# Two attention stages of a six-stage decoder on one core: layernorms cut into steps, a scale moved from the softmax sums into a copy, and one routing job sent at a time

## The chip, the cores and the metric

The kernel runs as one program on one core of a Trainium2 chip. The core has a matrix engine (PE, with its weight loads shown as PEld), a vector engine (DVE), a scalar engine (ACT), a GpSimd engine (POOL), a queue engine that starts most transfers (SP), and 16 DMA engines. Each engine takes its own instructions in order, and semaphores tie the engines together. The metric is the device time of one execution in microseconds (us); the smaller the better.

## What is computed

The reference is a post-norm decoder of two layers over x of 16 blocks x 128 tokens x 512 features: a state-space scan, a cross attention, a ternary feed-forward, a bit-linear self attention, a gated cross attention, and a mixture of experts. Each is followed by a residual sum and a layernorm:

```python
x = _layernorm(x + _L0_attn_ref(x, ...))      # scan
x = _layernorm(x + _L0_xattn_ref(x, ctx, ...))
x = _layernorm(x + _L0_ffn_ref(x, ...))
x = _layernorm(x + _L1_attn_ref(x, ...))      # 16 heads of 32, ternary weights, 8-bit activations
x = _layernorm(x + _L1_xattn_ref(x, ctx, mask, ...))   # 16 heads of 32, gated
x = _layernorm(x + _L1_ffn_ref(x, ...))       # 64 experts in 8 groups, top 8
```

The change lies in the fourth and fifth. The fifth, cut to what matters:

```python
q, k, v = heads of rmsnorm(x) @ wq.T, memory @ wk.T, memory @ wv.T
attn = softmax(where(mask, q k^T / sqrt(32), -inf));  attn = nan_to_num(attn, nan=0)
out  = (attn @ v) @ wo.T
return sigmoid(x @ wg.T) * out
```

A block whose memory tokens are all masked gives 0, which the kernel gets from a flag per block (`gated_any`, a [128, 16] tile named anyk in the profile). The sigmoid is computed as (1 + tanh) / 2, so a factor of one half stands somewhere in the kernel.

## The kernel before

Six stages follow one another: scan, cross attention, feed-forward, then `stage_attention`, which holds both small-head attentions, and `stage_moe`.

**The attention stage.** x lies in 16 tiles of 128 tokens (x0 to x15), taken in pairs. There are 8 pairs of `SelfAttention` and then 8 of `GatedAttention`, and each pair is worked in 8 units of four heads of a tile, 128 units in all. The loop at L1518 takes one step t per unit. Around step t it issues, for units at different lags: the score matmuls (`scores`, two steps ahead), the row maxima (`top`, one step ahead, L1442 and L1443 on DVE), the exponentials (`exps`, L1451 on ACT, four per unit, with their sums into sm), the division by the sums (`norm`, one step behind), the turn of the probabilities (`turn`: PE transposes pts at L536, and a copy at_T, on ACT at L1295 or on DVE at L1297), and after each four units the generator `values` of the tile. Generators are in the list `running`, and each is advanced once per step: `project` (transposes pt of x and the copies xT at L1380 and L1383 on DVE, queries, copy qT at L1411, gate at L1415 and L1420 on ACT), `values`, weight loads.

**One unit's division in the gated attention** (`norm`, L1455): DVE takes the reciprocal of sm, 128x4 (L1457), DVE multiplies it by the block's flag and by 0.5 (L1459), and POOL multiplies the 128x512 tile at_s by it (L1460).

**A tile's end in the gated attention** (`values`, L1464): PE makes ao from at_T and v (L1472), ACT copies it to oT (L1478), PE multiplies by the output weights into pw (L1482), DVE makes gate = (gate + 1) * pw (L1485), and POOL adds it to x (L1486). After the second tile of a pair, the layernorm of both tiles runs as one block (L1490): bn_stats (L101) and bn_aggr (L102) for both tiles, a reciprocal square root by Newton steps (L78 to L91), and two 128x512 multiplications (L105). Its instructions are given to a scheduler by `keep_in_program_order`.

**The order of instructions.** A scheduler of the framework places each engine's instructions before the program is built; what `keep_in_program_order` wraps keeps its place relative to the other wrapped instructions of the engine, the rest may move. So the order on an engine is fixed when the program runs, and an instruction whose input is late holds all behind it on its engine.

**Routing beside the gated attention.** When a pair of tiles of the first half has its layernorm, its number is appended to `to_route` (L1493). `Moe.tick`, called twice a step, advances one `route` job: transposes of x, gate logits, top 8, softmax and offsets, a chain of small DVE operations (L1675 to L1751). A routed pair then becomes a job of `sending`. `Moe.send`, called once a step, advances every job of that list: each advance issues two scatters of rows by POOL (L1760, an indirect DMA; 16 per pair, so 64 in all beside the attention). POOL thus carries L1460, L1486 and L1760 in one queue.

**Tiles with few buffers.** The transposes pts and pt share one PSUM buffer (`ppt`, bufs=1), ao and pw share one (`pao`), at_s has four.

**The experts.** `stage_moe` (from about 2183 us) runs the routed rows through gate, up and down matmuls; it calls `m.send` once a step for the pairs that were not sent before.

Of the kernel before, what the change touches and what calls it, by code (L numbers as in the profile page):

```python
# [10 lines left out]
F32 = mybir.dt.float32  # L11
BF16 = mybir.dt.bfloat16
F32R = mybir.dt.float32r
I32 = mybir.dt.int32
# [6 lines left out]
P = 128  # L21
# [11 lines left out]
class Homes:  # L33


    def __init__(self, **homes):
        self.homes = homes
# [57 lines left out]
def layernorm(k, ins, outs, eps=1e-5, keep=lambda ins: ins):  # L95

    nc, n = k.nc, len(ins)
    mv = k.small.tile([P, n, 2], F32, tag=f"ln_mv{n}", name="ln_mv")
    for i, r in enumerate(ins):
        st = k.small.tile([P, nc.vector.BN_STATS_DIM], F32, tag="ln_st", name="ln_st")  # L100
        keep(nc.vector.bn_stats(st, r))  # L101
        keep(nc.vector.bn_aggr(mv[:, i, :], st))  # L102
    rstd = rsqrt(k, mv[:, :, 1], n, eps, keep=keep)
    for i, (r, o) in enumerate(zip(ins, outs)):
        keep(nc.vector.tensor_scalar(o, r, mv[:, i, 0:1], rstd[:, i : i + 1], ALU.subtract, ALU.mult))  # L105


def stage_ssm(k):
# [981 lines left out]
def load_gated_masks(k, raws):  # L1090


    nc, a, pool = k.nc, k.args, k.bit_pool
    m8 = raws.tile([P, NB, P], U8, name="m8")
    nc.sync.dma_start(m8, a["mask"].rearrange("b t -> (b t)").partition_broadcast(P).rearrange("p (b t) -> p b t", b=NB))
    yield
    k.gated_any = pool.tile([P, NB], F32, name="anyk")
    k.tc.keep_in_program_order(nc.vector.tensor_reduce(k.gated_any, m8, AX.X, ALU.max))
    yield
    k.gated_mask = mb = pool.tile([P, NB, P], BF16, name="mb")  # L1100
    k.tc.keep_in_program_order(nc.vector.tensor_scalar(mb, m8, 1e30, -1e30, ALU.mult, ALU.add))
    yield
    k.tc.keep_in_program_order(nc.vector.tensor_tensor(mb, mb, k.gated_any.unsqueeze(2).to_broadcast([P, NB, P]), ALU.mult))
    yield


# [18 lines left out]
class SelfAttention:  # L1125
# [199 lines left out]

    def output(self):
        nc, k, y = self.nc, self.k, Ctx()
        yield from self.levels(self.o, y)
        step = y.step
        nc.vector.tensor_scalar(step, step, k.bit_sw[:, 1:2], None, ALU.mult)  # L1330
        yield
        for i in range(2):
            po = self.pp.tile([P, D], F32, tag="pp", name="po")
            for c in range(KC):
                nc.tensor.matmul(po, y.qT[:, KC * i + c], k.bit_w[:, c, 768:1280], start=c == 0, stop=c == KC - 1)
            yield
            nc.vector.scalar_tensor_tensor(self.xs[i], po, step[:, i : i + 1], self.xs[i], ALU.mult, ALU.add)
        yield
        layernorm(k, self.xs, self.xs)
        yield  # L1340


class GatedAttention:
# [109 lines left out]
            )  # L1453

    def norm(self, n):  # L1455
        nc, s, sm, b = self.nc, self.s[n], self.sm[n], self.b0 + n // 4
        nc.vector.reciprocal(sm, sm)  # L1457

        nc.vector.tensor_scalar(sm, sm, self.k.gated_any[:, b : b + 1], 0.5, ALU.mult, ALU.mult)  # L1459
        nc.gpsimd.tensor_tensor(s, s, sm.unsqueeze(2).to_broadcast([P, KC, P]), ALU.mult)  # L1460

    turn = SelfAttention.turn
# [1 line left out]
    def values(self, i):  # L1464
        yield
        nc, wk, k = self.nc, self.wk, self.k
        ao = self.pao.tile([P, KC, P], F32, tag="ao", name="ao")
        side = Side(k)
        for c in range(KC):
            for r in (3, 0, 1, 2):  # L1470
                at = (4 * c + r) * self.HD
                side(nc.tensor.matmul(  # L1472
                    ao[32 * r : 32 * r + 32, c], self.v[i][:, at : at + self.HD], self.sT[4 * i + r][:, c * P : (c + 1) * P],
                    start=True, stop=True,
                ))
        yield
        oT = wk.tile([P, KC, P], F32, tag="aoT", name="oT")
        nc.scalar.copy(oT, ao)  # L1478
        yield
        pw = self.pao.tile([P, D], F32, tag="ao", name="pw")  # L1480
        for c in range(KC):
            nc.tensor.matmul(pw, oT[:, c], k.gated_w["wo"][:, c], start=c == 0, stop=c == KC - 1)  # L1482
        yield
        gt = self.gate[i]
        k.tc.keep_in_program_order(nc.vector.scalar_tensor_tensor(gt, gt, 1.0, pw, ALU.add, ALU.mult))  # L1485
        nc.gpsimd.tensor_tensor(self.xs[i], self.xs[i], gt, ALU.add)  # L1486
        yield
        if i == 1:
            yield
            layernorm(k, self.xs, self.xs, keep=k.tc.keep_in_program_order)  # L1490
            yield
            if self.b0 < NB // 2:
                k.to_route.append(self.b0 // 2)  # L1493


def stage_attention(k):

    nc, tc = k.nc, k.tc
    U = 8
    with ExitStack() as ctx:
        wk = ctx.enter_context(tc.tile_pool(name="s4w", bufs=2))
        own = ctx.enter_context(ExitStack())
        wr = own.enter_context(tc.tile_pool(name="s4r", bufs=2, side="right"))
        pp = ctx.enter_context(tc.tile_pool(name="s4p", bufs=2, space=PSUM))
        psc = ctx.enter_context(tc.tile_pool(name="s4s", bufs=1, space=PSUM))
        ppt = ctx.enter_context(tc.tile_pool(name="s4t", bufs=1, space=PSUM))
        pao = ctx.enter_context(tc.tile_pool(name="s4o", bufs=1, space=PSUM))  # L1510
        pools = wk, wr, pp, psc, ppt, pao
        pairs = [c(k, p, pools) for c in (SelfAttention, GatedAttention) for p in range(NB // 2)]
        pairs[0:2] = k.bit_first
        for pr in pairs[0:2]:
            pr.take(pools)
        units = [(pr, n) for pr in pairs for n in range(U)]

        begin = {}  # L1518
        for m, pr in enumerate(pairs):
            begin.setdefault(U * m - (14 if m < NB // 2 else 10), []).append(pr)  # L1520
        running = [load_gated_weights(k), k.bit_second]
        for t in range(-2, len(units) + 2):
            if k.moe:
                k.moe.tick()
            for lag in (2, 1, 0, -1, -2):
                if not 0 <= t - lag < len(units):
                    continue
                pr, n = units[t - lag]
                if lag == pr.LAG:
                    pr.turn(n)  # L1530
                    if n % 4 == 3:
                        running.append(pr.values(n // 4))
                if lag == 1:
                    pr.norm(n)
                if lag == 0:
                    pr.exps(n)
                if lag == -1 and n % 2 == 0:
                    pr.top(n)
                if lag == -2 and n % 2 == 0:
                    pr.scores(n)  # L1540
            if t == NB // 2 * U + 20:
                own.close()
                k.moe = Moe(k, pp)
                running.append(k.moe.setup())
            for pr in begin.get(t, []):
                if t > -2:
                    running.append(pr.project())
            for job in list(running):
                if next(job, running) is running:
                    running.remove(job)  # L1550
            if k.moe:
                k.moe.tick()
                k.moe.send()
            if t == len(units) - 8:
                assert not (k.moe.now or k.moe.sending or k.to_route)
                running.append(k.moe.open())
        while running:
            k.moe.tick()
            for job in list(running):
                if next(job, running) is running:  # L1560
                    running.remove(job)
            k.moe.tick()
            k.moe.send()


class Moe:
# [22 lines left out]

    def send(self):  # L1590

        for job in list(self.sending):
            if next(job, self) is self:
                self.sending.remove(job)

    def setup(self):

# [275 lines left out]
def stage_moe(k):  # L1873
# [4 lines left out]
    with ExitStack() as ctx:  # L1878
# [25 lines left out]
        for t in range(-3, len(units) + 4):  # L1904
# [23 lines left out]
            advance()  # L1928
            m.tick()
            m.send()  # L1930
            if t == 60:

                full = k.small.tile([1, NG], F32, tag="full", name="full", bufs=1)
                most = k.small.tile([1, 1], F32, tag="most", name="most", bufs=1)
                flag = k.small.tile([1, 1], I32, tag="flag", name="flag", bufs=1)
                nc.vector.tensor_tensor(full, m.off[0][0:1], m.off[1][0:1], ALU.max)
                nc.vector.tensor_reduce(most, full, AX.X, ALU.max)
                nc.vector.tensor_scalar(flag, most, float(m.CAP), None, ALU.is_gt)
                over = nc.values_load(flag, min_val=0, max_val=1)
# [146 lines left out]
```

## Time and profile before

| | us |
|---|---|
| median of 3 runs | 3029.26 (3026.57 to 3032.8) |
| the profiled execution | 3033.7 |
| its span | 3031.8 |
| mean granted PE clock | 0.992 |

The span by stretches, busy time of each engine in us (the profile's windows; DVE 174.51 in the first row means 174.51 us of 194):

| stretch | us | PE | DVE | ACT | POOL | PE clock |
|---|---|---|---|---|---|---|
| self attention, 1672 to 1866 | 194 | 178.31 | 174.51 | 170.90 | 118.23 | 0.97 |
| gated attention, 1866 to 2182 | 316 | 296.87 | 211.57 | 177.64 | 152.39 | 0.98 |
| start of the experts, 2182 to 2240 | 58 | 55.64 | 30.08 | 19.45 | 9.52 | 0.97 |
| experts, 2240 to 3031 | 791 | 781.07 | 238.53 | 182.37 | 313.61 | 1.00 |

In a list of groups, "x64 | 22.6, 356" means 64 instructions, 22.6 us busy in all, 356 ns mean of one; what follows the second bar is the idle time of the engine just before them, and what ended it. In a timeline each line gives the start in us, the duration in us, engine, source line, operation and tile names, and in brackets the idle time before it with what released it. The granted clock (PEclk) is the share of full speed at which PE was allowed to run.

### The profile page before, as it was taken

How to read it: one execution, taken by the hardware profiler on the slowest of the kernel's cores; microseconds unless marked ns; L12 is line 12 of the kernel's file. 1: busy time of each engine (PE TensorE's matmuls, PEld its weight loads, DVE VectorE, ACT ScalarE, POOL GpSimd, SP SyncE). 2: the span in 40 equal slices, each digit the busy share in tenths (PEclk: the TensorE clock that was granted, in tenths of full speed). 3: DMA queues.
4: the chain of work that ended last, by engine and by line, in shares of the span. 5: the costliest groups of instructions: out<-in, count | busy, mean ns of one | idle time of the engine just before them, and what ended most of it. 6: DMA issues, size and time to landing. Idle time of an engine off the chain costs nothing.

```text
span 3031.8 us, 40699 instructions
## 1 busy us (share of the span) xinstructions
PE 2927.2 (97%) x13744; PEld 1830.9 (60%) x13744; DVE 1920.5 (63%) x4221; ACT 1356.5 (45%) x3315; POOL 1490.4 (49%) x1274
## 2 busy tenths in 40 slices
PE   8999999999999999999999999999999999999998
PEld 6666665455555555555787556666566666666665
DVE  6989998766776676665887897567643322242224
ACT  5776775333343343345344797655433322222221
POOL 8999996534334334332333663356435553333331
PEclk9999999999999999999999999999999999999999
DMA  6654444880000000024000200234357665555541
GB/s 199 205 138 126 121 126 135 266 285 14 8 11 11 8 11 11 8 66 143 1 1 1 70 1 8 64 115 164 136 174 241 221 226 164 165 192 165 164 150 61
DMA packets 171603, 331.58 MB, mean 109 GB/s; under 512 B 22078, under 2 KB 80958, under 8 KB 169852
## 3 DMA queue, kind: packets, MB, share of 16 engines
q1 hardware_dynamic: 126988, 219.91, 23.9%
q0 software_dynamic: 19200, 64.16, 6.3%
q10 hardware_dynamic: 25200, 44.84, 3.9%
q8 instruction: 111, 1.82, 0.2%
q14 instruction: 104, 0.85, 0.1%
HBM read 244.57 MB, written 137.43 MB: 126 GB/s over the span
## 4 chain that ended last, share of the span: by engine, by line
PE 67%; DVE 13%; ACT 3%; POOL 1%; issue 1%; DMA 1%; SPq 0%; another core or an unknown queue 0%; DVEq 0%; ACTq 0%; POOLq 0%
PE y L1830 8%; PE pu L1813 7%; PE pg L1813 7%; PE pq L676 7%; PE po L796 6%; PE po L1008 4%; PE ao L785 3%; PE sc L745 3%; PE pt L536 2%; PE pg L988 2%; PE pu L988 2%; PE pT L773 1%; PE ptx L536 1%; PE pkv L66 1%; PE pw L1482 1%
## 5 line engine op out<-in xcount | busy, mean ns | idle before, releaser
L765 POOL TENSOR_TENSOR pr<-pr,sm 128x512 f32<-128x512 f32 x128 | 135.4, 1058 | 369.2 <-DVE sm L764 273.8
L66 POOL TENSOR_TENSOR dBx<-dtx,BC 128x1024 f32<-128x1024 f32 x126 | 298.6, 2394 | 1.0 <-DMA BC<-bcd 0.4
L1813 PE MATMUL pg<-gu,xgT 128*128 128x352 f32 x784 | 297.1, 461 | 1.4 <-ACT act L1816 1.4
L1813 PE MATMUL pu<-gu,xgT 128*128 128x352 f32 x784 | 296.9, 460 | 0.0
L758 ACT ACTIVATE pr<-sc,mx,sf 128x256 f32<-128x256 f32 x256 | 142.2, 560 | 332.8 <-DVE mx L751 304.7
L1817 DVE SCALAR_TENSOR_TENSOR act<-pu,row,act 128x352 f32<-128x352 f32 x98 | 57.1, 582 | 358.4 <-PE pu L1813 339.2
L1830 PE MATMUL y<-dn,aT 128*128 128x512 f32 x588 | 268.3, 592 | 0.0
L1858 POOL TENSOR_TENSOR x<-got,x 128x512 f32<-128x512 f32 x120 | 151.7, 1270 | 225.8 <-DMA got<-results,gidx 224.6
L66 ACT ACTIVATE h<-dt,negA 128x254 f32<-128x254 f32 x508 | 242.2, 477 | 16.9
L796 PE MATMUL po<-w,aT 128*128 128x512 f32 x512 | 233.1, 593 | 1.9 <-DVE aT L790 1.9
L676 PE MATMUL pq<-w,xT 128*128 128x512 f32 x512 | 230.8, 593 | 0.6 <-DVE m L642 0.6
L1851 POOL DMA_INDIRECT got<-results,gidx x120 | 116.2, 969 | 227.6 <-DMA results<-yo 200.5
L66 DVE TENSOR_TENSOR_SCAN h<-h,dBx 128x1024 f32<-128x1024 f32 x80 | 183.2, 2290 | 34.3 <-ACT h L66 24.9
L1813 PEld LDWEIGHTS pu<-gu,xgT 128*128 128x128 f32 x784 | 149.3, 191 | 83.0 <-issue 0.5
L1816 ACT ACTIVATE act<-pg 128x352 f32<-128x352 f32 x98 | 45.5, 464 | 304.5 <-PE pg L1813 265.3
L1813 PEld LDWEIGHTS pg<-gu,xgT 128*128 128x128 f32 x784 | 141.6, 191 | 65.1 <-ACT act L1816 1.9
L647 POOL TENSOR_TENSOR m<-m,m 128x512 f32<-128x512 f32 x96 | 122.5, 1276 | 111.3 <-DVE m L642 108.0
L66 PE MATMUL pkv<-w,cT 128*128 128x512 f32 x384 | 171.6, 593 | 1.4 <-ACT y L66 1.1
L1842 DVE COPY yo<-y 128x512 f32<-128x512 f32 x90 | 62.2, 691 | 165.4 <-PE y L1830 157.9
L1830 PEld LDWEIGHTS y<-dn,aT 128*128 128x128 f32 x588 | 104.1, 190 | 100.8 <-issue 94.2
L1805 ACT COPY xgT<-ptx 128x512 f32<-128x512 f32 x98 | 57.4, 586 | 235.9 <-PE ptx L536 221.4
L998 POOL TENSOR_TENSOR lo<-sg,hi 128x512 fp32r<-128x512 f32 x64 | 84.2, 1316 | 155.4 <-ACT hi L997 155.3
(413 smaller groups left out, 6792.0 us busy)
## 6 DMA issues: line engine op xcount, KB each, us to landing
bucket<-zeros SPq DMA_DIRECT2D x96, 388.0 KB
row<-bucket SPq DMA_DIRECT2D x90, 388.0 KB
BC<-bcd SPq DMA_DIRECT2D x128, 256.0 KB
results<-yo ACTq DMA_DIRECT2D x90, 256.0 KB
gu<-in_moe_guT SPq DMA_DIRECT2D x16, 1408.0 KB
x_k<-kv ACTq DMA_DIRECT2D x32, 256.0 KB
x_v<-kv ACTq DMA_DIRECT2D x32, 256.0 KB
v<-x_v SPq DMA_DIRECT2D x32, 256.0 KB
```

What stands on the lines that cost most here:

```text
L66: return self.tc.keep_in_program_order(call(*args, **kw))
L647: nc.gpsimd.tensor_tensor(m1, m1, m2, ALU.add)
L676: nc.tensor.matmul(ps, src[:, c], w[c], start=c == 0, stop=c == KC - 1)
L758: nc.scalar.activation(pr[:, j], st.sc[g, i][:, j], AF.Exp, scale=st.sf[:, h : h + 1], bias=st.mx[g, i][:, j : j + 1], accum_out=sm[:, j : ...
L765: nc.gpsimd.tensor_tensor(pr, pr, sm.unsqueeze(2).to_broadcast([P, 2, 2 * P]), ALU.mult)
L796: nc.tensor.matmul(st.po, aT[:, j], k.wo[h // 8][:, h % 8], start=h == 0, stop=h == G * J - 1)
L988: nc.tensor.matmul(p[:, e], w[:, c, at : at + P], sn.qT[:, :, c], start=c == 0, stop=c == KC - 1)
L1008: nc.tensor.matmul(sn.po[i], part[:, e, i * P : (i + 1) * P], k.fd[hc // 8][:, hc % 8], start=hc == 0 and part is parts[0], stop=hc == 15 ...
L1813: nc.tensor.matmul(ps, u.xT[:, c], gu[:, c, lo : lo + I], start=c == 0, stop=c == KC - 1)
L1830: self.nc.tensor.matmul(u.y, u.aT[:, c], u.w[1][:, c], start=c == 0, stop=c == 2)
L1851: nc.gpsimd.indirect_dma_start(out=got[:, :], out_offset=None, in_=k.results[h][g][0:end, :], in_offset=bass.IndirectOffsetOnAxis(ap=self. ...
L1858: nc.gpsimd.tensor_tensor(k.x[b], got, k.x[b], ALU.add)
```

## The change

It has three parts.

1. **Norms in steps.** A class `Norm` takes the place of `layernorm` in both attentions. `stats(i)` issues bn_stats and bn_aggr of one tile; `finish()` is a generator: three Newton steps with a yield after each, then one multiplication per tile with a yield after each. In the self attention `stats` follows each tile's own sum; in the gated attention it follows two steps after the tile's gate and sum. The instructions are no longer wrapped. The pair is appended to `to_route` five steps later than before.
2. **The flag and the half.** L1459 is taken out. The flags are multiplied by 0.5 once, when they are loaded (one 128x16 operation), and the copy of ao to oT is a multiplication by the block's flag (a [128, 1] operand).
3. **Sending.** `Moe.send` advances the first job of the list alone. The attention loop calls it once a step, and twice from step 109 on; `stage_moe` calls it twice a step.

```diff
+class Norm:
+    def __init__(self, k, xs):
+        self.k, self.xs, n = k, xs, len(xs)
+        self.mv = k.small.tile([P, n, 2], F32, tag=f"ln_mv{n}", name="ln_mv")
+    def stats(self, i):
+        nc = self.k.nc
+        st = self.k.small.tile([P, nc.vector.BN_STATS_DIM], F32, tag="ln_st", name="ln_st")
+        nc.vector.bn_stats(st, self.xs[i])
+        nc.vector.bn_aggr(self.mv[:, i, :], st)
+    def finish(self):
+        nc, n, small = self.k.nc, len(self.xs), self.k.small
+        a, y, t = (small.tile([P, n], F32, tag=f"rs_{name}{n}", name="rs_" + name) for name in "ayt")
+        nc.vector.tensor_scalar(a, self.mv[:, :, 1], 1.0, 1e-5, ALU.mult, ALU.add)
+        nc.vector.tensor_scalar(y.bitcast(I32), a.bitcast(I32), -0.5, 1597463007.0, ALU.mult, ALU.add)
+        for _ in range(3):
+            nc.vector.tensor_tensor(t, y, y, ALU.mult)
+            nc.vector.scalar_tensor_tensor(t, t, -0.5, a, ALU.mult, ALU.mult)
+            nc.vector.scalar_tensor_tensor(y, t, 1.5, y, ALU.add, ALU.mult)
+            yield
+        for i, x in enumerate(self.xs):
+            nc.vector.tensor_scalar(x, x, self.mv[:, i, 0:1], y[:, i : i + 1], ALU.subtract, ALU.mult)
+            yield
...
+    k.tc.keep_in_program_order(nc.vector.tensor_scalar(k.gated_any, k.gated_any, 0.5, None, ALU.mult))
...
             nc.vector.scalar_tensor_tensor(self.xs[i], po, step[:, i : i + 1], self.xs[i], ALU.mult, ALU.add)
-        yield
-        layernorm(k, self.xs, self.xs)
-        yield
+            norm.stats(i)
+        yield
+        yield from norm.finish()
...
-        nc.vector.tensor_scalar(sm, sm, self.k.gated_any[:, b : b + 1], 0.5, ALU.mult, ALU.mult)
...
-        nc.scalar.copy(oT, ao)
+        nc.scalar.mul(oT, ao, k.gated_any[:, self.b0 + i : self.b0 + i + 1])
...
         nc.gpsimd.tensor_tensor(self.xs[i], self.xs[i], gt, ALU.add)
+        if i == 0:
+            self.norm_out = Norm(k, self.xs)
+        yield
+        yield
+        self.norm_out.stats(i)
         yield
         if i == 1:
-            yield
-            layernorm(k, self.xs, self.xs, keep=k.tc.keep_in_program_order)
-            yield
+            yield from self.norm_out.finish()
...
-                k.moe.send()
+                for _ in range(1 + (t > len(units) - 20)):
+                    k.moe.send()
...
-        for job in list(self.sending):
-            if next(job, self) is self:
-                self.sending.remove(job)
+        if self.sending and next(self.sending[0], self) is self:
+            self.sending.pop(0)
...
             m.tick()
+            m.send()
             m.send()
```

More of the change, by code (lines that the diff above doesn't have):

```diff
@@ L1327, in output @@
         nc, k, y = self.nc, self.k, Ctx()
+        norm = Norm(k, self.xs)
         yield from self.levels(self.o, y)
@@ L1455, in norm @@
     def norm(self, n):
-        nc, s, sm, b = self.nc, self.s[n], self.sm[n], self.b0 + n // 4
+        nc, s, sm = self.nc, self.s[n], self.sm[n]
         nc.vector.reciprocal(sm, sm)
-        nc.vector.tensor_scalar(sm, sm, self.k.gated_any[:, b : b + 1], 0.5, ALU.mult, ALU.mult)
         nc.gpsimd.tensor_tensor(s, s, sm.unsqueeze(2).to_broadcast([P, KC, P]), ALU.mult)
```

## The prediction, made before the change was run

> **What bounds the kernel now.** I read the stage windows first. In the gated attention, 1866 to 2182 us, PE is busy 296.87 of 316 us, DVE 211.57, ACT 177.64, POOL 152.39. In the self attention DVE is the limit (174.51 of 194, and 40.00 of 40 us between 1760 and 1800). In the experts PE is (781.07 of 791). The change touches the first two stages, and only the seams of the third. So in the gated attention a DVE or POOL instruction is worth what PE waits for it: 316 - 296.87 = 19.1 us. I listed the single gaps of PE (17.8 us in 17 places), then the waits of PE in this window, whose columns are total, times and longest:
>
> ```profile
> PE pts L536 <- ACT at_T L1295: 6.6, 4, 2.5
> PE pt L536 <- DVE xT L1380: 2.5, 2, 2.2
> PE pt L536 <- ACT at_s L1451: 1.7, 1, 1.7
> PE pg L1403 <- DVE qT L1411: 1.4, 1, 1.4
> PE pg L1403 <- DVE sm L1457: 1.2, 1, 1.2
> ```
>
> The reader is to see that the waits are few and short, and that none names the division by the sums on POOL. Then I read the groups of this window:
>
> ```profile
> L1459 DVE TENSOR_SCALAR sm<-sm,anyk 128x4 f32<-128x4 f32 x64 | 22.6, 356 | 1.0
> L1460 POOL TENSOR_TENSOR at_s<-at_s,sm 128x512 f32<-128x512 f32 x64 | 67.0, 1048 | 90.0 <-DVE sm L1459 36.2 <-DVE rs_y L87 9.2 <-DVE rs_t L89 8.4
> L1760 POOL DMA_INDIRECT bucket<-r_row,r_to x64 | 63.3, 990 | 34.9 <-issue 19.9 <-DVE r_row L1751 10.1 <-DVE gidx L1744 1.1
> L1478 ACT COPY oT<-ao 128x512 f32<-128x512 f32 x16 | 9.4, 588 | 22.7 <-PE ao L1472 16.6 <-PE pg L1403 4.0 <-PE pt L536 1.1
> L1420 ACT ACTIVATE gate<-pg,r 128x512 f32<-128x512 f32 x7 | 4.9, 701 | 3.4 <-PE pg L1403 2.3 <-issue 1.1
> ```
>
> L1459 is 22.6 us of DVE time, and DVE has 104 us free here. Last I read the timelines at the two longest gaps that DVE or ACT explains. PE, then DVE:
>
> ```profile
> 2107.64 0.49 PE L1436 MATMUL sc<-kT,qT 32*128 32x128 f32 x4
> 2110.36 0.66 PE L536 MATMUL pt<-ident,x 128*128 128x128 f32 x4 [2.23 <-DVE xT L1380]
> ...
> 2112.25 5.40 PE L1482 MATMUL pw<-x_wo,oT 128*128 128x512 f32 x8
> ```
>
> ```profile
> 2101.73 2.33 DVE L1459 TENSOR_SCALAR sm<-sm,anyk 128x4 f32<-128x4 f32 x1
> ...
> 2109.03 0.68 DVE L101 BATCH_NORM_STATS2 ln_st<-x 128x6 f32<-128x512 f32 x1
> 2109.63 0.67 DVE L1380 COPY xT<-pt 128x512 f32<-128x512 f32 x1
> ```
>
> xT stands behind an L1459 that took 2.33 us while POOL ran L1486 and L1460, behind the routing chain, a row maximum and a bn_stats. PE lost 2.23 us, and then ran at half clock: the eight pw took 5.40 us against 3.70 at 1944.48, 1.7 us more.
>
> **The change, part by part.** Sums are made against the profiled execution (3033.7 us, span 3031.8, so 1.9 outside it). It lies 4.4 us above the median of 3029.26. I apply the sum to the median.
>
> *Self attention.* In the built order of the changed kernel PE, ACT and POOL have the same order there; DVE's instructions move by one or two places with the same count. DVE is full, so its work counts, and that is unchanged: 0, bounds -1.5 to +1.5 (one bn_stats pair of 0.68 + 0.17 us, earlier or later, at a seam).
>
> *The place at 1942.84.* PE waited 2.54 us for at_T on ACT. ACT stood in an exponential (idle 2.61 us, released by the row maximum L1443), and DVE did that maximum behind three operations on the experts' weights. In the changed order at_T follows oT directly and the exponentials come after it; oT had ended at 1939.06, and pts were done by 1939.43. The gap goes: -2.5. Next late would be the scores, which need the same row maxima; the exponentials run three to four units ahead, so I charge nothing; without that cover the gap returns in whole.
>
> *The place at 2110.36.* The routing chain comes some five units later, and bn_stats no longer stands as a block ahead of xT: -2.2, and the half clock with it, -1.7; together -3.9.
>
> *Small gaps behind DVE.* 1.40 us at 1885.20 (qT behind L1457 and L1459), 0.57 at 2044.21 (the same), 1.21 at 2089.08 (sm), 0.85 at 1980.57 (xT): 4.0 us. One L1459 is 0.36 us on the mean, up to 2.33. Half goes: -2.0, bounds -4.0 and 0.
>
> *The place at 1902.37*, 1.36 us for at_T behind two exponentials, of which one now stands elsewhere: -0.7, bounds -1.4 and 0.
>
> *The bursts.* At 2004.23 and 2006.49 PE lost 3.8 us with the scatters on POOL, and 3.4 us more to half clock. ACT's oT waited there until pg had ended (2002.06). The scatters are as many as before, 64, each 0.99 us with 0.30 us behind it, 1.28 us. Sent one pair at a time they come in fours after t=109, and up to 12 stand between two divisions (12 x 1.28 + 1.27 for an L1486 = 16.6 us, where before L1460 waited up to 11 us). The end of L1460 lies 4 to 17 us ahead of the transposes that need it, so 16.6 - 11 = 5.6 us more would just use up the smallest. I take 0, bounds -7.2 (all of it gone) and +1.6 (5.6 - 4).
>
> *oT.* An ACTIVATE with a scale from a tile in place of a copy: the nearest row of the same 128x512 shape is the gate, 701 ns, against 588. 16 x 0.113 = 1.8 us on the chain ao, oT, pw. Half of it lies beside other transposes and scores: +0.9, bounds 0 and 1.8.
>
> *The flags.* One more 128x16 operation at the load, like L1706 of 128x16 (0.56 us on the mean); DVE has space and nobody waits: 0, bounds 0 and +0.6.
>
> *The wait that is added.* In the built order bn_stats now stands directly behind the gate L1485, and it needs x from L1486 on POOL, at least 1.27 us away; before, a row maximum, a copy and more stood between. Queued behind it on DVE: one reciprocal (for POOL's L1460), the Newton steps, at_T on DVE (PE waits for that: pts has one buffer) and the next maxima. For x5, x7, x9 and x11 L1486 itself stands behind eight scatters: 8 x 1.28 + 1.05 (L1460) + 1.27 = 12.5 us, begun about a unit (316/64 = 4.9 us) before the gate, so DVE waits up to 7.6 us. Cover: at_T goes to DVE every second unit, and one such copy stood just ahead of the gate, so the next is due 5 to 9 us after it. I take +1.5, bounds 0 and 4 x 3.6 = 14.4 (cover of 4 us alone).
>
> *The seam to the experts.* The first transfers of rows leave SP at 2180.60 behind the last L1486 of POOL. The same instructions stand there, without pinning: 0, bounds -1 and +1.
>
> Sum: -2.5 - 3.9 - 2.0 - 0.7 + 0.9 + 1.5 = -6.7 us. 3029.26 - 6.7 = **3022.6**.
>
> One rule is to be weighed. The Trainium skill, TensorE: Matmul & The Clock Gate, "What's actually happening", says that PE falls to half clock after at least one idle window of about 3.4 us. Here a gap of 2.23 us was followed by a granted clock of 0.66 over 2111 to 2116, and one of 2.54 us (1942.84) was not: the measurement speaks against the figure as a lower bound. By the rule the gap of 2110 would cost no clock, and the sum would be -5.0 us.
>
> **The rivals.** *A, as worked out:* 3022.6. For it: the gaps are in the trace, and the built order removes their causes. *A+, the bursts' loss goes too:* -6.7 - 7.2, and the other halves of the small gaps -2.0: -15.9 in all, 3013. For it: a job alone loads POOL with two scatters a step, never four at once before t=109. Against: 12 in a row. *B, nothing:* the gaps move to other places, since each queue has single buffers and PE is 94% busy; what is left is oT: 3030. For it: DVE is a third idle, and L1460 waits for nothing that PE then waits for. *C, slower:* bn_stats blocks DVE for 7.6 us at x5, x7, x9 and x11, PE stalls 3.6 us at each (14.4), and two half-clock windows follow (3.4). With the gains of 9.1 and oT's 0.9, +9.6 us: 3039. It decides from a block at which the four stalls equal the net gains, (9.1 - 0.9) / 4 = 2.1 us of stall, about 6 us of block. Against it: in the run before, POOL's delay of x let DVE wait 0.6 us in all, and at_T has up to 9 us.
>
> **How the numbers follow.** A 0.40, A+ 0.18, B 0.20, C 0.22. About 0.2% (6 us) is what a measurement of this kernel can tell from no change. A is centred at that edge: 0.27 of it beyond, 0.13 within. Faster 0.27 + 0.18 = 0.45; same 0.13 + 0.20 = 0.33; slower 0.22. The range takes in A+ with its bounds (-15.9, and 4 more for the bounds of the rest) and C without its worst: 3009 to 3038.
>
> **What would show it.** Right: no gap of PE near the first routing with at_T on ACT as releaser, none over 1 us with xT; DVE some 22 us less busy; oT near 0.70 us. Wrong: waits of DVE's ln_st (bn_stats) on POOL's x of 5 us and more, with PE gaps released by DVE's at_T beside them; runs of scatters with PE waiting for at_s; more stretches of half clock in the gated attention. The prediction fails if PE's idle time there is above 19 us.

## The result, and the profile after

The changed kernel takes 3040.01 us (median of 6 runs, 3037.05 to 3044.44) against 3029.4 (6 runs, 3026.57 to 3032.8): a ratio of 1.0036, 95% interval 1.0026 to 1.0046, so slower by 10.6 us. Forecast were 3022.6, a gain of 6.7. The profiled execution took 3038.36 us (span 3036.6), 1.7 us under its median; that of before lay 4.3 us above its own. So the two profiles are only 4.7 us apart, and the medians decide on sizes.

DVE has 21.7 us less work on the page (1898.8 against 1920.5). The waits of DVE from 1866 to 2196 us in the profile after, in total, times and longest:

```profile
DVE sm L1488 <- ACT at_s L1482: 51.2, 33, 2.5
DVE ln_st L118 <- POOL x L1515: 29.8, 15, 4.4
DVE gate L1514 <- PE pw L1511: 16.1, 6, 4.2
```

The second line is new: before, ln_st (bn_stats) waited once for POOL's x, 0.6 us:

```profile
DVE ln_st L101 <- POOL x L1486: 0.6, 1, 0.6
```

It now does so 15 times. In the same stretch, the largest waits of PE:

```profile
PE pts L565 <- DVE at_T L1327: 4.8, 4, 1.7
PE pt L565 <- DVE xT L1411: 4.7, 3, 2.0
PE pts L565 <- POOL at_s L1489: 2.7, 1, 2.7
```

PE's releasers changed from ACT to DVE and POOL, but the idle time did not grow: over 1866 to 2196 us it is 330 - 310.46 = 19.5 us against 330 - 308.51 = 21.5. What grew is time at half clock. Here is this stretch before, then after (columns: PE, PEld, DVE, ACT and POOL busy with instructions, granted clock, DMA share, GB/s):

```profile
1866.00:2196.00 330.00, 308.51 (x2093) 201.12 (x2092) 218.18 (x689) 181.09 (x641) 152.39 (x150) 0.97 0.31 109
1866.00:2196.00 330.00, 310.46 (x2060) 201.31 (x2058) 195.26 (x621) 179.94 (x632) 150.62 (x148) 0.95 0.30 104
```

Adding (1 - granted clock) times the width over windows of 2 us gives 17.1 us lost against 8.5. Four stretches of the profile after hold 15.3 of it:

```profile
2012.00:2026.00 14.00, 11.37 (x41) 6.80 (x41) 8.71 (x27) 6.18 (x26) 7.74 (x8) 0.63 0.37 145
2060.00:2070.00 10.00, 8.11 (x31) 4.96 (x32) 7.00 (x21) 5.74 (x25) 5.88 (x6) 0.66 0.34 134
2104.00:2114.00 10.00, 8.10 (x32) 4.92 (x32) 8.16 (x20) 4.63 (x19) 6.87 (x7) 0.66 0.36 141
2146.00:2156.00 10.00, 9.13 (x34) 5.37 (x35) 8.11 (x8) 5.17 (x22) 8.65 (x9) 0.66 0.58 224
```

They lie behind the ends of tiles 5, 7, 9 and 11. At the first, POOL, then DVE, then PE:

```profile
2002.27 1.06 POOL L1489 TENSOR_TENSOR at_s<-at_s,sm 128x512 f32<-128x512 f32 x1
2003.49 1.01 POOL L1792 DMA_INDIRECT bucket<-r_row,r_to  x1 [0.17 <-issue]
2004.81 0.97 POOL L1792 DMA_INDIRECT bucket<-r_row,r_to  x1 [0.30 <-issue]
2005.79 1.30 POOL L1515 TENSOR_TENSOR x<-x,gate 128x512 f32<-128x512 f32 x1
```

```profile
2002.23 0.66 DVE L1514 SCALAR_TENSOR_TENSOR gate<-gate,pw 128x512 f32<-128x512 f32 x1
2007.12 0.69 DVE L118 BATCH_NORM_STATS2 ln_st<-x 128x6 f32<-128x512 f32 x1 [4.23 <-POOL x L1515]
...
2009.97 1.66 DVE L90 SCALAR_TENSOR_TENSOR rs_t<-rs_t,rs_a 128x2 f32<-128x2 f32 x1
...
2011.75 0.54 DVE L133 TENSOR_SCALAR x<-x,ln_mv,rs_y 128x512 f32<-128x512 f32 x1
...
2012.41 0.61 DVE L133 TENSOR_SCALAR x<-x,ln_mv,rs_y 128x512 f32<-128x512 f32 x1
2012.95 0.67 DVE L1327 COPY at_T<-pts 128x512 f32<-128x512 f32 x1
```

```profile
2010.50 1.90 PE L1703 MATMUL pl<-gw,r_x 128*128 128x64 f32 x16
2013.77 0.63 PE L565 MATMUL pts<-ident,at_s 128*128 128x128 f32 x4 [1.36 <-DVE at_T L1327]
2015.66 1.11 PE L565 MATMUL pt<-ident,x 128*128 128x128 f32 x4 [1.27 <-DVE xT L1411]
```

POOL makes the sum L1515 only after its queue of scatters. DVE stands 4.23 us, then does the statistics, the whole Newton chain, with that of another pair's projection (L86 to L91) between its steps, and both multiplications (2007.12 to 2012.95), and only then the copy at_T that PE needs. One step of 128x2, L90, took 1.66 us of this, where its neighbours take 0.16; it ended 0.02 us after a POOL division that began at 2010.53. At all four places:

| tile | DVE waits for POOL's sum | PE idle after it | lost to half clock |
|---|---|---|---|
| 5 | 4.23 us | 1.36 + 1.27 | 5.1 |
| 7 | 4.44 | 0.85 + 1.96 | 3.4 |
| 9 | 3.48 | 1.46 + 0.43 | 3.4 |
| 11 | 2.71 | 2.70 (POOL's division, late behind scatters) | 3.4 |

### The profile page after: what moved, and what is told of

It reads as the page before. It is cut to its first block, busy times and chain, and to the rows that moved or that the text cites. A ratio compares the mean times of both kernels' runs of the same rounds, so it can differ in the third digit from the quotient of the medians.

```text
span 3036.6 us, 40550 instructions
## 1 busy us (share of the span) xinstructions
PE 2931.3 (97%) x13744; PEld 1833.7 (60%) x13744; DVE 1898.8 (63%) x4158; ACT 1360.1 (45%) x3315; POOL 1489.7 (49%) x1274
## 4 chain that ended last, share of the span: by engine, by line
PE 66%; DVE 13%; POOL 3%; ACT 2%; issue 2%; DMA 1%; SPq 0%; POOLq 0%; ACTq 0%; DVEq 0%
PE y L1862 8%; PE pu L1845 7%; PE pg L1845 7%; PE pq L705 7%; PE po L825 6%; PE po L1037 3%; PE ao L814 3%; PE sc L774 3%; PE pt L565 2%; PE pg L1017 2%; PE pu L1017 2%; PE pT L802 1%; PE ptx L565 1%; PE pkv L66 1%; PE ps L1428 1%
```

## The experiments

Ratios are to the kernel before on the same chip, with their 95% intervals. To place the time within a profile, the middle of the kernel is cut at the at_T copies: "gated" is from unit 64 to unit 124, "rest" from there to PE's last matmul. The kernel before has 287.7 and 856.1 us, the changed one 293.8 and 856.8. Each such figure is of one execution: e13 below has the attention of the changed kernel, untouched, and 301.4. A difference of under some 8 us between two "gated" figures therefore says little by itself.

**e1: the sum on DVE.**

```diff
-        nc.gpsimd.tensor_tensor(self.xs[i], self.xs[i], gt, ALU.add)
+        nc.vector.tensor_tensor(self.xs[i], self.xs[i], gt, ALU.add)
```

> The changed kernel with one edit: the residual sum x + gate of the gated attention is done by DVE in place of POOL, so the statistics behind it no longer wait for POOL; the scatters stay as they are. Theory 'the wait': the loss comes from the statistics waiting 4.2 to 4.4 us for POOL's sum behind the scatters at tiles 5, 7 and 9, PE then pausing 1.4 to 2.0 us and running at half clock for some 7 us after each. It expects 3029 us or less (3040 less three times about 3.5 us), no PE gap over 1 us near the first three routings, and one gap left where 12 scatters stand in a row. Rival 'the bursts': scatters delay the divisions by the sums on POOL, and so PE. It expects 3037 to 3040 and the gaps where they were. Rival 'the copy': the scaled copy of the turned outputs costs; it expects 3040.

Measured: 3026.02 against 3026.31, ratio 0.9998 (0.9988 to 1.0008); gated 283.7. Some 0.38% of the changed kernel's ratio goes, 11 us. In e1's profile the wait on POOL is gone from DVE's list, and the half clock with it at the first two places:

```profile
2006.00:2020.00 14.00, 12.74 (x116) 8.87 (x115) 13.08 (x42) 5.76 (x21) 11.04 (x11) 1.00 0.48 175
2050.00:2060.00 10.00, 9.68 (x78) 6.56 (x70) 9.07 (x23) 5.00 (x19) 7.97 (x9) 1.00 0.56 215
2096.00:2106.00 10.00, 8.57 (x31) 5.14 (x32) 6.00 (x20) 6.19 (x26) 4.38 (x5) 0.66 0.24 94
2137.00:2147.00 10.00, 7.41 (x42) 4.12 (x44) 3.85 (x9) 6.41 (x26) 8.50 (x9) 1.00 0.56 221
```

At the third place it stays, 3.4 us lost as in the changed kernel: xT is late there without any wait for POOL's sum. A pause for qT comes in, too, with 1.7 us of half clock behind it:

```profile
2074.06 1.25 PE L1434 MATMUL pg<-x_wg,xT 128*128 128x512 f32 x2 [1.73 <-DVE qT L1442]
2096.83 0.66 PE L565 MATMUL pt<-ident,x 128*128 128x128 f32 x4 [1.07 <-DVE xT L1411]
```

At the fourth place PE pauses twice for POOL's division, 1.73 and 1.99 us, at no cost in clock.

**e2: the gated norm as one block again.**

```diff
-        if i == 0:
-            self.norm_out = Norm(k, self.xs)
-        yield
-        yield
-        self.norm_out.stats(i)
         yield
         if i == 1:
-            yield from self.norm_out.finish()
+            yield
+            layernorm(k, self.xs, self.xs, keep=k.tc.keep_in_program_order)
+            yield
```

> The changed kernel with the gated attention's layernorm put back as one wrapped block (the self attention's norm, the flag and the sending stay changed). Theory 'the wait': a row maximum and a copy stand again between the gate and the statistics, so DVE waits for POOL less than 1 us in all; 3023 to 3030 us. Rival 'the bursts': sending one job at a time, twice a step from 109 on, is still there; 3035 to 3040. Rival 'the copy': 3038 to 3040.

Measured: 3022.0 against 3026.31, 0.9988 (0.9979 to 0.9998); gated 276.4; the statistics waited 2.6 us in all:

```profile
DVE ln_st L101 <- POOL x L1515: 2.6, 3, 1.9
```

So the spread norm of the gated attention, with the later routing that it brings, costs 1.0036 - 0.9988 = 0.48%, over 14 us.

**e3: the flag back in the sums.**

```diff
+        nc.vector.tensor_scalar(sm, sm, self.k.gated_any[:, b : b + 1], 0.5, ALU.mult, ALU.mult)
-        nc.scalar.mul(oT, ao, k.gated_any[:, self.b0 + i : self.b0 + i + 1])
+        nc.scalar.copy(oT, ao)
```

> The changed kernel with the flag and the half put back into the sums (64 small DVE operations more, a plain copy of the turned outputs). Theory 'the wait': the loss stays, 3039 to 3046, since DVE has more work behind its waits. Rival 'the copy': 3030. Rival 'the bursts': 3040.

Measured: 3044.77 against 3026.31, 1.0060 (1.0047 to 1.0073); gated 296.7. The loss is there without the scaled copy, and is larger, as the theory has it: half clock takes 20.5 us from 1866 to 2196 us.

**e4: the flag and the half alone** (the reverse of e3's diff, on the kernel before).

> The kernel before with the second part alone: no multiplication of the sums by flag and half, the copy of the turned outputs scaled by the flag. Theory 'the wait': this part is a gain, 3022 to 3029 against 3029 before. Rival 'the copy': 16 scaled copies are on PE's chain, 3032 or more.

Measured: 3023.83 against 3026.31, 0.9990 (0.9981 to 0.9999): a gain of 2.5 us (0.3 to 5.7 by the interval). The profiled execution, with gated 277.9, lies 4.2 us below the median.

**e5 and e6: without the scatters**, in the changed kernel and in the one before:

```diff
             for g in range(self.NG - half):
-                nc.gpsimd.indirect_dma_start(...)
+                if half:
+                    nc.gpsimd.indirect_dma_start(...)
```

> The changed kernel without the 64 scatters of rows beside the gated attention (work left out: the experts of the first half get empty buckets; all else runs). It tells whether the place of the statistics behind the gate is enough for the loss, or whether the scatters ahead of POOL's sum are needed. Theory 'the wait behind scatters': DVE's waits for POOL's sum fall from 4.2 to 4.4 us to 1.2 to 1.9 each, PE keeps its pace; the gated stage from its first to its last turn takes 12 us or more less than in the changed kernel, in all about 3026. Rival 'the place alone': statistics, Newton steps and the two multiplications stand as a block ahead of the turns' copies; three PE gaps with half clock stay, 3034 or more.

> The kernel before without the same 64 scatters (the same work left out): what the scatters cost where the statistics stand later. Theory 'the wait behind scatters': little, 3022 to 3029, as nothing there waits for POOL's sum. If the scatters alone are dear by their time on POOL or by their traffic, 3016 or less, and then the run without scatters of the changed kernel proves less.

Measured: e5 3037.84 against 3032.39, 1.0014 (1.0005 to 1.0024); e6 3019.24, 0.9955 (0.9940 to 0.9971). By the totals, "the place alone" won. The profile says otherwise: gated is 271.8 in e5 and 273.9 in e6, but rest is 880.8 in e5, with PE gaps of 7.28 and 8.26 us in the experts' stage that neither kernel has. So the totals do not decide; e9 has that stage as before. e6 fell below what was expected: the scatters cost the kernel before some 13 us, about as much as the gated stage is shorter (287.7 to 273.9).

**e7 and e8: the sending alone, and the self attention's norm alone,** on the kernel before (the last three groups of lines of the change's diff; the class `Norm` and the lines of the self attention's `output`).

> The kernel before with the third part alone: the first job of the list is sent, twice a step from step 109 on, twice a step in the experts' stage. All theories that blame the wait: within 3 us of the kernel before, 3026 to 3032, since no two jobs stood in the list at one time and only the last two run twice as fast. Rival 'the bursts': 3032 or more, with PE waiting for the divisions on POOL behind rows of scatters near the last two jobs.

> The kernel before with the first part in the self attention alone: statistics after each sum, Newton steps and multiplications spread. DVE bounds that stage and its work is the same: 0 to -2 us against before, by 1.5 us at the seams. If spreading were bad in itself, +3 or more.

Measured: e7 3049.98 against 3032.39, 1.0061 (1.0047 to 1.0075), a miss of all that blamed the wait alone. Gated is 289.0, rest 874.0: the loss is in the experts' stage, not in the attention. e8 3032.05, 0.9996 (0.9987 to 1.0006): nothing.

**e9: e5 with one send a step in the experts' stage.**

```diff
             m.tick()
             m.send()
-            m.send()
             if t == 60:
```

> The changed kernel without the 64 scatters beside the gated attention (the same work left out as before) and with one send a step in the experts' stage, as before the change. In the run without scatters the gated stage was short (272 us from unit 64 to unit 124, 294 in the changed kernel), but PE had three gaps of 2 to 8 us in the experts' stage. Theory 'the wait behind scatters, and the second send in the experts' stage is a cost of its own': the gaps there go, and the time is that of the kernel before without scatters or 2 us less, about 3017 where before is 3030. Rival 'the place alone': 3034 or more. Rival 'the gaps of the experts' stage have another cause': gaps of 7 us stay there, 3035.

Measured: 3019.74 against 3034.18, 0.9948 (0.9928 to 0.9968); gated 271.8, rest 856.9. It agrees with e6's ratio within the intervals: without the scatters the changed attention costs nothing. Its statistics still wait 15 times, but each less than 2 us, and from 1866 us on PE has no half clock before 2169:

```profile
DVE ln_st L118 <- POOL x L1515: 22.7, 15, 1.9
```

**e10, e11: the sending's two halves apart,** on the kernel before: `Moe.send` and the attention loop, or a second `m.send()` in `stage_moe`.

> The kernel before with the sending changed in the attention alone (first job only, twice a step from step 109 on), one send a step in the experts' stage. If the 18 us of the whole sending part come from the experts' stage: 3027 to 3033 where before is 3030. If from the attention: 3045.

> The kernel before with a second send a step in the experts' stage and nothing else. Only the order on POOL moves: scatters come ahead of 16 sums of gathered rows. If that is the cause of the gaps: 3045 or more, with PE gaps of 2 to 8 us between 2260 and 2490 us. If these come only with the doubled sends of the attention: 3030.

Measured: e10 3037.3 against 3034.18, 1.0015 (1.0003 to 1.0026), gated 290.7; e11 3050.22, 1.0054 (1.0037 to 1.0070), rest 876.7. So e7's loss is, all or most of it, the second send in the experts' stage. PE there in e11:

```profile
2471.34 2.74 PE L1830 MATMUL y<-dn,aT 128*128 128x512 f32 x6
2482.95 1.08 PE L536 MATMUL ptx<-ident,xg 128*128 128x128 f32 x4 [8.87 <-DVE xg L1799]
```

**e12: the flag and the self attention's norm,** on the kernel before.

> The kernel before with the second part and the self attention's half of the first: no spread norm in the gated attention, sending as before. It is the sum of what was a gain: 3024 to 3028 where before is 3030, the best of all. If the gated attention's spread norm were worth something beside its wait: no better than 3030.

Measured: 3032.97 against 3034.18, 0.9991 (0.9981 to 1.0001), gated 287.0. This agrees with e4, though the interval just takes in no change; the best of all it is not (e2, e15).

**e13: the changed kernel with e9's edit alone.**

> The changed kernel with one send a step in the experts' stage, as before the change; its attention is untouched. If a part of the loss comes from the second send there (18 us in the runs that sent twice without the scaled copy): 3022 to 3028 where before is 3030. If all of it comes from the wait in the gated attention, as its profile says: 3037 to 3041, with the half-clock stretches of the gated attention as before.

Measured: 3044.95 against 3033.55, 1.0031 (1.0019 to 1.0044); gated 301.4, rest 856.5. The loss stays, so no part of it is seen to come from the second send.

**e14: flag and sending together,** on the kernel before.

> The kernel before with the second and the third part: the scaled copy and the whole sending, no norm spread. The sending alone lost 18 us in the experts' stage; the same with the scaled copy and the self attention's norm lost nothing. If the scaled copy's shorter DVE queue is what protects: 3024 to 3028 where before is 3030. If the self attention's norm does, or the place of the code: 3045.

Measured: 3049.7 against 3033.55, 1.0045 (1.0032 to 1.0059); rest 875.0. The scaled copy does not protect. e2 has the same order of instructions from unit 124 on, on every engine, sends twice, and has a rest of 856.6; it differs from e14 in the self attention's norm alone. But e5 has that norm too, and lost. What decides is open.

**e15: e4 with the sum on DVE** (wrapped in `keep_in_program_order`).

> The kernel before with the second part and the residual sum of the gated attention on DVE: a version that might beat both kernels. POOL is rid of 20 us between the scatters, DVE gets some 11 us of the 22 us that the flag freed. Theory 'the wait' (POOL's place in DVE's queue is the risk): 3022 to 3027 where before is 3030. If DVE's own load counts: 3030 or more.

Measured: 3025.13 against 3033.55, 0.9969 (0.9957 to 0.9981), 8.4 us faster than before: of all versions with the whole computation the best against its own reference, and faster than both kernels. On POOL the sums no longer stand between the scatters. Against e4 the move of the sum gives some 0.2%, in a kernel without the wait; the intervals meet at 0.9981, and the two ran on different chips.

## Why the prediction was wrong

**The wait that was added** is the step that failed. It was priced at +1.5 us, with 14.4 as the upper end; by e2, which takes the spread norm of the gated attention out and leaves the rest, it and the later routing cost 0.48%, over 14 us. The place, the instruction and the queue were right: statistics directly behind the gate, tiles 5, 7, 9 and 11, eight scatters ahead of POOL's sum. The block was shorter than feared (2.7 to 4.4 us, not 7.6), but the cover was not what I took it for. at_T was due 5 to 9 us after the gate, and I set the block alone against that. The Newton chain and the multiplications had moved with the statistics and stood ahead of at_T too; the prediction names the Newton steps in that queue and does not add their time. At tile 5, at_T started 10.1 us after the gate had ended (2002.89 to 2012.95), 4.2 of it the block. PE's pauses behind tiles 5, 7 and 9 came to 7.3 us; those 2.70 us behind tile 11 ended with POOL's division and belong to the bursts. And **half clock** I charged once with 1.7 us, and in the slower rival with 3.4 in all; it took 15.3 us at the four places, 11.9 of them at the first three.

So the rival called slower (3039, chance 0.22) came true by its place and its direction. That its size is so near is in part luck: it counted 14.4 us of stalls and 3.4 of half clock, where the trace has 10.0 and 15.3. The point from which it decides, given as 6 us of block, lay lower: the blocks were 4.23, 4.44 and 3.48 us at the first three. The sign by which the prediction was to fail, PE's idle time above 19 us, did not come: from 1866 to 2182 us it is 16.5 us, against 19.1 before. It watched the pauses, and the loss lay in the clock. The other sign, more stretches of half clock, came.

What is shown: the loss needs the spread norm of the gated attention, with the later routing that it brings (e2), and it needs the scatters (e9 against e6). That it works by the wait is read from the rows at tiles 5, 7 and 9, where DVE stands idle for POOL's sum and PE then for DVE's copy; e1 bears this out at tiles 5 and 7. e1 does not prove it alone. Its edit also takes 16 sums off POOL's queue, which gives some 0.2% where nothing waits (e15 against e4), so about half of e1's 0.38% may be that. And e1 is 0.29% above e15 (on another chip), which has its sum on DVE too: without the wait a part of the cost stays, as at tile 9. How much each has of the 0.48%, no run shows. What narrows it: in e9 the routing runs as late as in the changed kernel, the statistics stand at the same place, and waits of up to 1.9 us behind the gate come without half clock. So it is what the scatters do on POOL, delay the sum or delay the divisions; and for a division PE waited once in the changed kernel, those 2.70 us.

The other terms, by the profiles, each of one execution:

- The place at 1942.84: -2.5 forecast, -0.9 came; the pause is 1.66 us at 1936.15 and now waits for at_T on DVE. The cause on ACT went, the next late one took its place.
- The place at 2110.36: -3.9 forecast, lost. xT was late after three of the four blocks.
- Small gaps: -2.0 forecast; of 4.0 us, 0.85 is left, so -3.2. One was misread: at 2044.21 L1459 stood behind qT, not ahead of it.
- The place at 1902.37: -0.7 forecast, -0.6 came (0.74 us left), and its half clock went.
- The bursts: 0 forecast. Those of 2004 are gone in this execution. Behind the row of 12 scatters one division came late, and PE paused 2.70 us for it, to 2146.87, with 3.4 us of half clock after it; the upper bound of 1.6 us was too low. The cover was misread: in the profile before, 13 of the 64 divisions end less than 4 us ahead of the first transpose that needs them, the nearest 0.06 us. e1, with a row of scatters and two such pauses there, lost no clock.
- oT: 689 ns on the mean against 588, near the gate's row of 701; e4 gains in spite of it, and what it costs by itself no run shows.
- Self attention: e8 shows no change. The seam: rest +0.6 us.

So the gains were about as large as forecast up to unit 92, where the changed kernel's profile is 8.8 us ahead; from unit 92 to unit 120 it loses 14.6 us. These are two single executions, and e13 shows how far one can lie from another. That removing L1459 is a gain was right (e4), but 2.5 us of it by the medians. That sending one job at a time would gain by itself, as rival A+ had it, was not seen: e10, with this and the doubling from step 109 on, is 0.15% slower. Which of the two costs is not separated.

One rule of the Trainium skill was weighed in the prediction: TensorE: Matmul & The Clock Gate, "What's actually happening", lets PE fall to half clock after an idle window of about 3.4 us. The runs speak against it as a lower bound: no pause at the four places was longer than 2.70 us, and each place was followed by some 7 to 10 us at a granted clock of 0.5. Nor does the length of a pause decide: 1.66 us at 1936.15, and 1.73 and 1.99 us at e1's fourth place, cost no clock.

## What to carry to other kernels

Before an instruction that waits for a slower engine is moved up on a queue that feeds the bound engine, count what stands ahead of its producer on the producer's queue, and what moves along behind the waiting instruction, not the wait alone. Where the bound engine loses clock after a pause, price a pause above its length: at the four places here 10.0 us of pauses were followed by a loss of 15.3 us more, 2.5 times in all, though other pauses cost no clock. And test each part of a change alone: here the part that looked like a detail, a second send a step in the experts' stage, cost more by itself, on the kernel before, than the whole change.

## What the hardware did that was not expected

A short DVE instruction can be held for as long as POOL works on a tile. In e2, DVE's 128x8 multiplication, then POOL:

```profile
2049.36 3.17 DVE L1474 TENSOR_SCALAR mx<-mx,r 128x8 f32<-128x8 f32 x1
```

```profile
2049.21 1.30 POOL L1515 TENSOR_TENSOR x<-x,gate 128x512 f32<-128x512 f32 x1
2050.43 2.06 POOL L1489 TENSOR_TENSOR at_s<-at_s,sm 128x512 f32<-128x512 f32 x2
```

It mostly takes 0.23 us where POOL is not at work on a tile, and here 3.17, to 2052.53; POOL's three operations end at 2052.49. In the kernel before, ten of the 64 L1459 took 0.66 to 2.33 us, each ending 0.02 to 0.04 us after an operation of POOL. The Trainium skill, GPSIMD Engine Reference, "Specifications", says that GpSimd's SBUF interfaces are shared with VectorE and that some of VectorE's instructions contend with it there. The rows agree with that, though no run shows whether these operations are of the kind that it names; and they give a price, here the whole of POOL's work.

And the experts' stage can lose 18 to 25 us (rest of 874 to 881 us against 856) when scatters are sent twice a step. In e11, near 2475 us, ACT stood idle for 9.4 us, PE for 8.9 and DVE for 13.0, while POOL issued one scatter or gather after the other. e2, with e14's order on all queues from unit 124 on, runs through that stage without a pause of 1.5 us or more, and so does the changed kernel. Why is not settled.
